# Head steps at half slots in a new order, tap responses in twenty chunks, and an eighth product with B on GpSimd

## The chip, the cores and the metric

The kernel runs on one core of one Trainium2 chip. The metric is the device time of one execution in microseconds (us). Lower is better.

## What is computed

The input is one image `x` of shape (1, 64, 256, 128): 64 channels, 256 time steps, 128 frequencies, in fp32. Two layers follow one another.

Layer 0 is a pair of bidirectional Mamba blocks, first along time (128 sequences of 256), then along frequency (256 sequences of 128). Every direction does this:

```python
xz = rmsnorm(u) @ in_proj.T ; x, z = split(xz)             # 128 + 128 wide
x  = silu(causal_conv4(x) + conv_b)
dt, B, C = split(x @ x_proj.T)                             # 4, 16, 16
dt = softplus(dt @ dt_proj.T + dt_b)
h  = exp(dt * A) * h + dt * B * x                          # scan, 128 x 16 states
y  = (h @ C + x * Dp) * silu(z)
out = y @ out_proj.T + u
```

The two directions are joined by a linear layer and added to the input.

Layer 1 normalises over the whole image (one mean and one deviation), runs a convolutional LSTM over 32 windows of 8 time steps in two directions, projects back, applies two PReLUs and adds the residual. The mean of the image enters the convolutions of layer 1 only through the response of each convolution tap to the norm's gain and bias; these "tap responses" need weights alone, so they can be made while layer 0 still runs.

## The kernel before

**Tiling.** `Stage` does one axis of layer 0: stage 0 along time, stage 1 along frequency. A stage has 64 chunks of 512 tokens. A chunk has two directions `d`, and a direction has 16 state groups of 128 rows, taken two at a time. Such a pair is one step `S` of the loop in `Stage.run`, so a chunk has 16 steps and a stage 1024. `where(S)` gives chunk, direction and group.

**One pair** (tiles of 128 partitions x 1024 fp32) goes through these methods:

- `inputs`: TensorE spreads `dtx` (dt times x) over the states into PSUM, tile `bx` (three buffers), line 445.
- `decays`: ScalarE takes `exp(A * dt)` from the loaded tile `rep` into SBUF, tile `dA` (line 468), and clears the column in front of each sequence (line 465).
- `times_b`: VectorE multiplies `bx` by B in place, in PSUM (line 480).
- `recur`: VectorE scans (line 490) into `h` (five buffers).
- `outputs`: GpSimd multiplies `h` by C (line 503).
- `add_up`: TensorE sums `h` over the states into `y` (line 512), once for two pairs.

For the pairs in `SWAPPED` (numbers within 32 pairs, two chunks) the two operands of the scan change places: ScalarE copies `bx` from PSUM into the `dA` tile (line 462) and puts the decays into the `bx` tile, and GpSimd does the product with B in SBUF (line 477). The scan then reads the decays from PSUM.

**The head.** What a chunk needs before its first pair is a list of steps, `HEAD`, written out by hand: each entry is a slot, a method's name and its arguments. Slot 16 is the chunk's own first step; slot 0 is 16 steps ahead of it. Slots below 0 and above 15 overlap with the neighbouring chunks. `load`, `squares`, `means`, `rms` and `normalise` make the normed input; `project_x`, `project_z` and `silus` make x and z of both directions; `project_bc` and `spread_bc` send B and C through DRAM to be spread over partitions; `softplus_a`, `softplus_b`, `softplus_sum` make dt; `dt_away` writes it to DRAM and eight `spread_dt` load it back, spread, into the `rep` tiles (seven buffers, `NREP`); `times_x` makes `dtx` on GpSimd (line 395).

**Order.** The schedule is manual: each engine runs its instructions in the order in which the program issues them, and each DMA here is issued by the SP queue in that same order. Within step `S` the program issues `times_b(S+1)`, `recur(S)`, the `gate` of a direction when it is done (line 528), `outputs(S-1)`, `inputs(S+2)`, `decays(S+2)`; then the head steps of that slot; then `skip`, `add_up`, `close_a`, `close_b`, `keep`. All projections, the softplus and the responses share one PSUM buffer, the tag "mm".

**Tap responses.** In stage 1 `Gates.fetch` loads the weights of one tap of one direction (512 KB, tile `w`, one buffer) at slot 10, and at slot 6 of the next chunk `Gates.respond` multiplies them with gain and bias: eight matmuls of two columns (line 707), which the profile records as sixteen, and one ScalarE copy into `made` (line 710). Ten chunks have one.

**After layer 0** `ConvLstm.prepare` combines weights and `ConvLstm.run` does the 32 LSTM steps. The change does not touch them.

Of the kernel before, what the change touches and what calls it, by code (L numbers as in the profile page):

```python
# [36 lines left out]
P = 128  # L37
# [19 lines left out]
HALF = T // 2  # L57
NRING = 4
NREP = 7
NH = 5  # L60
LAG = 2
SWAPPED = (3, 5, 10, 14, 19, 26, 29)
EXP_AND_LN = "natural_log_exp_and_others"
SILU = "silu_and_others"
EDGES = (0, 1, LF - 2, LF - 1)
# [1 line left out]


HEAD = (
    (-11, "load"),  # L70
    (-7, "squares"),
    (-5, "means"),
    (-5, "rms"),
    (-3, "normalise"),
    (0, "project_x", 0),
    (1, "project_z", 0),
    (4, "project_x", 1),
    (5, "project_z", 1),
    (5, "silus"),
    (6, "project_bc", 0),  # L80
    (8, "softplus_a", 0),
    (8, "softplus_b", 0),
    (10, "spread_bc", 0, 0),
    (10, "softplus_sum", 0),
    (12, "dt_away", 0),
    (12, "spread_bc", 0, 1),
    (12, "spread_dt", 0, 0),
    (12, "times_x", 0),
    (12, "spread_dt", 0, 1),
    (12, "project_bc", 1),  # L90
    (12, "spread_dt", 0, 2),
    (13, "softplus_a", 1),
    (13, "softplus_b", 1),
    (14, "spread_dt", 0, 3),
    (15, "spread_dt", 0, 4),
    (15, "softplus_sum", 1),
    (15, "spread_dt", 0, 5),
    (15, "spread_dt", 0, 6),
    (15, "spread_bc", 1, 1),
    (18, "dt_away", 1),  # L100
    (18, "spread_dt", 0, 7),
    (19, "spread_dt", 1, 0),
    (20, "spread_bc", 1, 0),
    (20, "spread_dt", 1, 1),
    (20, "times_x", 1),
    (22, "spread_dt", 1, 2),
    (22, "spread_dt", 1, 3),
    (23, "spread_dt", 1, 4),
    (26, "spread_dt", 1, 5),
    (27, "spread_dt", 1, 6),  # L110
    (27, "spread_dt", 1, 7),
)


# [118 lines left out]
class Stage:  # L233
# [8 lines left out]
    def __init__(self, ctx, m, stage, L, X, src, moments, gates):  # L242
# [8 lines left out]
        self.wk = ctx.enter_context(tc.tile_pool(name=n + "wk", bufs=1))  # L251
        self.st = ctx.enter_context(tc.tile_pool(name=n + "st", bufs=NH))
        self.dram = ctx.enter_context(tc.tile_pool(name=n + "dram", bufs=3, space=bass.MemoryType.DRAM))
# [162 lines left out]
    def spread_dt(self, ch, d, n):  # L416
        k, r = divmod(n, 2)
        t = self.wk.tile([P, 2, NTOK], F32, name="rep", tag="rep", bufs=NREP)
        there = self.at["there", ch, d]
# [28 lines left out]
    def swapped(self, S):  # L448


        return S % 32 in SWAPPED

# [125 lines left out]
    def run(self):  # L578
        nch = NCH
        last = 16 * nch  # L580
        silu = next(slot for slot, name, *_ in HEAD if name == "silus")
        steps = {}
        for ch in range(nch):
            for slot, todo in self.head(ch).items():
                steps.setdefault(16 * (ch - 1) + slot, []).extend(todo)
        for S in range(min(steps), last + LAG + 4):
            if 0 <= S + 1 < last:
                self.times_b(S + 1)
            if 0 <= S < last:
                self.recur(S)  # L590
            if S % 8 == LAG and S > 8:
                self.gate(*self.where(S - 8)[:2])
            if 0 < S <= last:
                self.outputs(S - 1)
            if 0 <= S + 2 < last:
                self.inputs(S + 2)

            for ahead in ((2, 3) if S % 16 == silu else () if S % 16 == silu + 1 else (2,)):
                if 0 <= S + ahead < last:
                    self.decays(S + ahead)  # L600
            for f, args in steps.get(S, []):
                f(*args)
            if S % 8 == LAG and 0 < S < last:
                self.skip(*self.where(S)[:2])
            if (S - LAG) % 2 and LAG < S <= last + LAG:
                self.add_up(S - LAG)
            if S % 16 == LAG and S > 16:
                self.close_a(S // 16 - 1)
            if S % 16 == LAG + 1 and S > 16:
                self.close_b(S // 16 - 1)  # L610
                self.keep(S // 16 - 1)
            if not self.time and S > 16:
                if S == last + LAG + 2:
                    self.spread_of(nch - 1)
                elif S % 16 == 14 and S < last:
                    self.spread_of(S // 16 - 1)

                n = S // 16 - 1
                if n < 10 and S % 16 == 10:
                    self.gates.fetch(n, self.io)  # L620
                if 0 < n < 11 and S % 16 == 6:
                    self.gates.respond(n - 1, self.mm("made"))


class Moments:
# [47 lines left out]
class Gates:  # L673
# [24 lines left out]
        self.w = pool.tile([P, 4, 256], F32, name="w", tag="w")  # L698
        self.nc.sync.dma_start(out=self.w, in_=self.d[("W_ih_f", "W_ih_b")[n // 5]][:, n % 5])

    def respond(self, n, pm):
        nc = self.nc
        half, k = divmod(n, 5)
        for gate in range(2):
            to = pm[:, 2 * gate : 2 * gate + 2]
            for j in range(4):
                nc.tensor.matmul(
                    to, lhsT=self.w[:, j, gate * P : (gate + 1) * P], rhs=self.gb, start=j == 0, stop=j == 3
                )
        nc.scalar.copy(  # L710
            self.made[:, 2 * half : 2 * half + 2, k], pm[:, 0:4].rearrange("p (g i) -> p g i", g=2)
        )


class ConvLstm:
# [449 lines left out]
```

## Time and profile before

| | before |
|---|---|
| median of 3 runs | 7435.62 us (7434.42 to 7440.39) |
| profiled execution | 7439.22 us, span 7437.4 us, mean TensorE clock 0.977 |
| VectorE (DVE) busy | 6987.4 us, 94% of the span |
| GpSimd (POOL) busy | 6558.7 us, 88% |
| TensorE (PE) busy | 6526.3 us, 88% (ends are modelled) |
| ScalarE (ACT) busy | 5999.8 us, 81% |
| first scan of stage 0 / stage 1 | 72.0 us / 3395.3 us |
| LSTM part | from about 6751 us to the end |

A line of the page's groups names the line of the code, the engine, the operation, the tile written and the tiles read, their sizes and how often; after the bar stand the busy time and the mean of one instruction in ns, and after the second bar how long the engine stood idle just before these instructions and which instruction ended most of that wait. A line of the timeline has the start and the length in us. A line of stretches has, for each engine, the busy time and in brackets the number of instructions, then the granted TensorE clock, the DMA share and the rate.

### The profile page before, as it was taken

The numbers are of one execution on the slowest core, as the hardware profiler recorded it, in microseconds if no ns is written. First come the engines' busy times: TensorE is split into PE (matmuls) and PEld (weight loads), VectorE is DVE, ScalarE is ACT, GpSimd is POOL, SyncE is SP. The second block draws the span as 40 slices with busy tenths as digits, with TensorE's granted clock in tenths as the row PEclk, the third lists the DMA queues.
The fourth block names the chain that finished last, engine by engine and source line by source line (L and its number), as shares of the span: only waits on it lengthen the run. The fifth ranks groups of instructions, "written<-read, shape, count | busy, mean of one in ns | idle before, by whom it ended". The sixth has DMA issues, their size and how long they took to land. (4 is left out here: it accounts for less than half of the span.)

```text
span 7437.4 us, 86153 instructions
## 1 busy us (share of the span) xinstructions
PE 6526.3 (88%) x25104; PEld 2203.8 (30%) x25104; DVE 6987.4 (94%) x4740; ACT 5999.8 (81%) x10892; POOL 6558.7 (88%) x3348
## 2 busy tenths in 40 slices
PE   7888888888888888887888888888888888888999
PEld 2222222222222222222222222222222222225887
DVE  6999999999999999996888999999999999996887
ACT  6888888888888888877777889888888888884333
POOL 5999999999999999996888999999999999995554
PEclk9999999999999999998999999999999999999999
DMA  5887888887888888876777877777777878782000
GB/s 148 207 208 205 205 210 204 207 207 202 206 207 204 206 205 205 206 185 163 190 184 186 204 201 202 203 208 201 201 204 202 208 197 205 205 203 72 15 15 16
DMA packets 509540, 1359.97 MB, mean 183 GB/s; under 512 B 75376, under 2 KB 133392, under 8 KB 509072
## 3 DMA queue, kind: packets, MB, share of 16 engines
q1 hardware_dynamic: 509072, 1354.46, 71.4%
q8 instruction: 205, 3.36, 0.2%
q14 instruction: 263, 2.15, 0.1%
HBM read 1228.34 MB, written 92.27 MB: 178 GB/s over the span
## 5 line engine op out<-in xcount | busy, mean ns | idle before, releaser
L503 POOL TENSOR_TENSOR h<-h,C 128x1024 f32<-128x1024 f32 x2048 | 4795.1, 2367 | 137.7 <-DVE h L490 120.1
L490 DVE TENSOR_TENSOR_SCAN h<-dA,bx 128x1024 f32<-128x1024 f32 x1600 | 3602.3, 2271 | 7.7 <-ACT dA L468 7.7
L445 PE MATMUL bx<-dtx,sel 64*128 64x512 f32 x8192 | 2368.3, 654 | 205.9 <-DVE h L490 205.7
L480 DVE TENSOR_TENSOR bx<-bx,B 128x1024 f32<-128x1024 f32 x1600 | 1940.8, 1213 | 251.0 <-PE bx L445 250.7
L468 ACT ACTIVATE dA<-rep,A 128x510 f32<-128x510 f32 (+1 forms) x3200 | 2117.0, 710 | 9.2 <-DMA rep<-there 6.0
L477 POOL TENSOR_TENSOR dA<-dA,B 128x1024 f32<-128x1024 f32 x448 | 1057.0, 2359 | 294.1 <-ACT dA L462 284.5
L445 PEld LDWEIGHTS bx<-dtx,sel 64*128 64x128 f32 x8192 | 640.4, 188 | 1857.4 <-issue 1045.8
L512 PE MATMUL y<-h,fold 128*32 128x512 f32 x8192 | 1119.0, 614 | 14.3 <-POOL h L503 7.6
L490 DVE TENSOR_TENSOR_SCAN h<-bx,dA 128x1024 f32<-128x1024 f32 x448 | 1021.0, 2279 | 2.5 <-POOL dA L477 1.3
L462 ACT COPY dA<-bx 128x1024 f32<-128x1024 f32 x448 | 450.7, 1006 | 251.3 <-PE bx L445 251.3
L468 ACT ACTIVATE bx<-rep,A 128x510 f32<-128x510 f32 (+1 forms) x896 | 617.4, 689 | 29.4 <-ACT bx L465 0.2
L401 PE MATMUL pb<-xs,xbc 128*32 128x512 f32 x512 | 291.4, 654 | 287.8 <-ACT xs L349 239.5
L327 ACT ACTIVATE xs<-px,cb 128x512 f32<-128x512 f32 x256 | 175.9, 687 | 372.9 <-PE px L326 372.9
L512 PEld LDWEIGHTS y<-h,fold 128*32 128x32 f32 x8192 | 167.3, 109 | 788.3 <-issue 432.0
L395 POOL TENSOR_TENSOR dtx<-dt,xs 128x512 f32<-128x512 f32 x256 | 326.8, 1276 | 62.2 <-ACT dt L383 62.2
L325 PE MATMUL px<-unp,g 128*128 128x512 f32 x512 | 292.7, 653 | 78.2 <-ACT X L561 35.8
L379 PE MATMUL pv<-w,ident 128*128 128x512 f32 x512 | 276.9, 623 | 91.1 <-ACT w L371 91.1
L358 PE MATMUL pv<-xs,wdt 128*128 128x512 f32 x512 | 290.0, 648 | 67.1 <-ACT bc L403 59.4
L379 PE MATMUL pv<-e,ident 128*128 128x512 f32 x512 | 290.0, 648 | 11.1 <-ACT e L362 7.8
L332 PE MATMUL pz<-unp,wz 64*128 64x512 f32 x512 | 268.2, 603 | 3.2 <-ACT xs L327 3.1
L326 PE MATMUL px<-unp,g 128*128 128x512 f32 x512 | 266.2, 601 | 0.0
L379 PE MATMUL pv<-lw,ident 128*128 128x512 f32 x512 | 262.7, 595 | 0.0
(190 smaller groups left out, 6887.6 us busy)
## 6 DMA issues: line engine op xcount, KB each, us to landing
rep<-there SPq DMA_DIRECT2D x2048, 512.0 KB
B<-away SPq DMA_DIRECT2D x256, 256.0 KB
there<-dt SPq DMA_DIRECT2D x1024, 64.0 KB
C<-away SPq DMA_DIRECT2D x256, 256.0 KB
unp<-xn SPq DMA_DIRECT2D x512, 64.0 KB
away<-bc SPq DMA_DIRECT2D x256, 64.0 KB
u<-in_x SPq DMA_DIRECT2D x128, 64.0 KB
out<-y SPq DMA_DIRECT2D x32, 256.0 KB
```

Source lines behind the costliest of these rows:

```text
L325: nc.tensor.matmul(self.seqs(px), lhsT=m.G1[i], rhs=self.unp[:, :, first : first + L], start=True, stop=False)
L379: nc.tensor.matmul(pv, lhsT=self.m.ident, rhs=t, start=False, stop=n == len(parts) - 1, skip_group_check=True)
L395: self.nc.gpsimd.tensor_mul(dtx, self.at["dt", d], self.at["xs", ch, d])
L401: self.nc.tensor.matmul(pb, lhsT=self.m.Wbc[2 * self.stage + d], rhs=self.at["xs", ch, d], start=True, stop=True)
L445: self.nc.tensor.matmul(bx[:, j], lhsT=self.m.sel[rows, r, k], rhs=dtx[rows], start=True, stop=True)
L462: nc.scalar.copy(dA.rearrange("p j n l -> p j (n l)"), bx)
L468: nc.scalar.activation(dA[:, j, :, live], self.seqs(rep[:, j])[:, :, live], AF.Exp, scale=m.A[:, i, g : g + 1])
L477: self.nc.gpsimd.tensor_mul(bx, bx, b)
L480: self.nc.vector.tensor_mul(bx, bx, b)
L490: self.nc.vector.tensor_tensor_scan(h.rearrange("p j n -> p (j n)")[:, step], dA[:, step], bx[:, step], 0.0, ALU.mult, ALU.add,)
L503: self.nc.gpsimd.tensor_mul(h, h, self.at["C", ch, d].unsqueeze(1).to_broadcast([P, 2, NTOK]))
L512: nc.tensor.matmul(y[32 * r : 32 * r + 32], lhsT=m.fold[:, k], rhs=hs[r % 2][:, r // 2], start=False, stop=k == NK - 1, skip_group_check=True,
```

## The change

`Stage.run` gets a second place for head steps, at the end of a step, after `keep`: an entry with slot `s + 0.5` is issued there. Many entries of `HEAD` are moved to other slots and some change order (`project_z` of the second direction now comes before its `project_x`; `project_bc` of the first goes from slot 6 to 7.5). `SWAPPED` has eight pairs instead of seven, at other places. `respond` does one gate at a time, four matmuls and one copy, at slot 6 of twenty chunks; `fetch` moves from slot 10 of ten successive chunks to slot 6 of every other chunk, after the response.

```diff
--- before.py
+++ after.py
@@ -57,9 +57,10 @@
 HALF = T // 2
 NRING = 4
 NREP = 7
+RESPOND = 6
 NH = 5
 LAG = 2
-SWAPPED = (3, 5, 10, 14, 19, 26, 29)
+SWAPPED = (2, 5, 9, 14, 18, 21, 25, 30)
 EXP_AND_LN = "natural_log_exp_and_others"
 SILU = "silu_and_others"
 EDGES = (0, 1, LF - 2, LF - 1)
@@ -67,48 +68,48 @@
 
 
 HEAD = (
-    (-11, "load"),
-    (-7, "squares"),
-    (-5, "means"),
-    (-5, "rms"),
+    (-13, "load"),
+    (-8.5, "squares"),
+    (-4.5, "means"),
+    (-4.5, "rms"),
     (-3, "normalise"),
     (0, "project_x", 0),
-    (1, "project_z", 0),
-    (4, "project_x", 1),
-    (5, "project_z", 1),
+    (1.5, "project_z", 0),
+    (4, "project_z", 1),
+    (5, "project_x", 1),
     (5, "silus"),
-    (6, "project_bc", 0),
+    (7.5, "project_bc", 0),
     (8, "softplus_a", 0),
-    (8, "softplus_b", 0),
-    (10, "spread_bc", 0, 0),
-    (10, "softplus_sum", 0),
-    (12, "dt_away", 0),
+    (8.5, "softplus_b", 0),
+    (8.5, "spread_bc", 0, 0),
+    (10.5, "softplus_sum", 0),
+    (10.5, "dt_away", 0),
+    (11.5, "times_x", 0),
     (12, "spread_bc", 0, 1),
     (12, "spread_dt", 0, 0),
-    (12, "times_x", 0),
     (12, "spread_dt", 0, 1),
-    (12, "project_bc", 1),
-    (12, "spread_dt", 0, 2),
+    (12.5, "project_bc", 1),
+    (12.5, "spread_dt", 0, 2),
     (13, "softplus_a", 1),
     (13, "softplus_b", 1),
-    (14, "spread_dt", 0, 3),
-    (15, "spread_dt", 0, 4),
+    (13.5, "spread_dt", 0, 3),
+    (14.5, "spread_dt", 0, 4),
     (15, "softplus_sum", 1),
-    (15, "spread_dt", 0, 5),
-    (15, "spread_dt", 0, 6),
-    (15, "spread_bc", 1, 1),
-    (18, "dt_away", 1),
-    (18, "spread_dt", 0, 7),
-    (19, "spread_dt", 1, 0),
-    (20, "spread_bc", 1, 0),
-    (20, "spread_dt", 1, 1),
-    (20, "times_x", 1),
-    (22, "spread_dt", 1, 2),
+    (15.5, "dt_away", 1),
+    (16, "spread_dt", 0, 5),
+    (16.5, "spread_dt", 0, 6),
+    (16.5, "spread_dt", 0, 7),
+    (17, "spread_dt", 1, 0),
+    (17.5, "spread_bc", 1, 0),
+    (19, "spread_dt", 1, 1),
+    (20.5, "times_x", 1),
+    (21, "spread_dt", 1, 2),
     (22, "spread_dt", 1, 3),
+    (23, "spread_bc", 1, 1),
     (23, "spread_dt", 1, 4),
-    (26, "spread_dt", 1, 5),
-    (27, "spread_dt", 1, 6),
-    (27, "spread_dt", 1, 7),
+    (24, "spread_dt", 1, 5),
+    (26.5, "spread_dt", 1, 6),
+    (26.5, "spread_dt", 1, 7),
 )
 
 
@@ -583,7 +584,7 @@
         for ch in range(nch):
             for slot, todo in self.head(ch).items():
                 steps.setdefault(16 * (ch - 1) + slot, []).extend(todo)
-        for S in range(min(steps), last + LAG + 4):
+        for S in range(int(min(steps)), last + LAG + 4):
             if 0 <= S + 1 < last:
                 self.times_b(S + 1)
             if 0 <= S < last:
@@ -609,6 +610,8 @@
             if S % 16 == LAG + 1 and S > 16:
                 self.close_b(S // 16 - 1)
                 self.keep(S // 16 - 1)
+            for f, args in steps.get(S + 0.5, []):
+                f(*args)
             if not self.time and S > 16:
                 if S == last + LAG + 2:
                     self.spread_of(nch - 1)
@@ -616,10 +619,11 @@
                     self.spread_of(S // 16 - 1)
 
                 n = S // 16 - 1
-                if n < 10 and S % 16 == 10:
-                    self.gates.fetch(n, self.io)
-                if 0 < n < 11 and S % 16 == 6:
-                    self.gates.respond(n - 1, self.mm("made"))
+                if S % 16 == RESPOND:
+                    if 0 < n < 21:
+                        self.gates.respond(*divmod(n - 1, 2), self.mm("made"))
+                    if n < 20 and n % 2 == 0:
+                        self.gates.fetch(n // 2, self.io)
 
 
 class Moments:
@@ -698,18 +702,14 @@
         self.w = pool.tile([P, 4, 256], F32, name="w", tag="w")
         self.nc.sync.dma_start(out=self.w, in_=self.d[("W_ih_f", "W_ih_b")[n // 5]][:, n % 5])
 
-    def respond(self, n, pm):
+    def respond(self, n, gate, pm):
         nc = self.nc
         half, k = divmod(n, 5)
-        for gate in range(2):
-            to = pm[:, 2 * gate : 2 * gate + 2]
-            for j in range(4):
-                nc.tensor.matmul(
-                    to, lhsT=self.w[:, j, gate * P : (gate + 1) * P], rhs=self.gb, start=j == 0, stop=j == 3
-                )
-        nc.scalar.copy(
-            self.made[:, 2 * half : 2 * half + 2, k], pm[:, 0:4].rearrange("p (g i) -> p g i", g=2)
-        )
+        for j in range(4):
+            nc.tensor.matmul(
+                pm[:, 0:2], lhsT=self.w[:, j, gate * P : (gate + 1) * P], rhs=self.gb, start=j == 0, stop=j == 3
+            )
+        nc.scalar.copy(self.made[:, 2 * half + gate, k], pm[:, 0:2])
 
 
 class ConvLstm:
```

## The prediction

> **What bounds the kernel now.** I read the page's busy line first, then its costliest groups, then the busy time in stretches of the span, then the timeline around the places where VectorE stands still.
>
> ```profile
> PE 6526.3 (88%) x25104; PEld 2203.8 (30%) x25104; DVE 6987.4 (94%) x4740; ACT 5999.8 (81%) x10892; POOL 6558.7 (88%) x3348
> ...
> L503 POOL TENSOR_TENSOR h<-h,C 128x1024 f32<-128x1024 f32 x2048 | 4795.1, 2367 | 137.7 <-DVE h L490 120.1
> L490 DVE TENSOR_TENSOR_SCAN h<-dA,bx 128x1024 f32<-128x1024 f32 x1600 | 3602.3, 2271 | 7.7 <-ACT dA L468 7.7
> L480 DVE TENSOR_TENSOR bx<-bx,B 128x1024 f32<-128x1024 f32 x1600 | 1940.8, 1213 | 251.0 <-PE bx L445 250.7
> L477 POOL TENSOR_TENSOR dA<-dA,B 128x1024 f32<-128x1024 f32 x448 | 1057.0, 2359 | 294.1 <-ACT dA L462 284.5
> L462 ACT COPY dA<-bx 128x1024 f32<-128x1024 f32 x448 | 450.7, 1006 | 251.3 <-PE bx L445 251.3
> ```
>
> VectorE leads, GpSimd is next. Over the whole span this is an average; the stretches separate it (busy time of PE, weight loads, VectorE, ScalarE, GpSimd with instruction counts, then granted clock, DMA share, GB/s):
>
> ```profile
> 1500.00:2000.00 500.00, 443.92 (x1662) 121.10 (x1660) 492.28 (x299) 434.75 (x774) 474.52 (x220) 0.98 0.81 206
> 3500.00:4000.00 500.00, 430.08 (x1600) 137.03 (x1604) 433.66 (x261) 390.00 (x726) 419.02 (x194) 0.92 0.73 188
> ```
>
> In the first, VectorE is busy 492 of 500 us: it is the bound. In the second it loses 66 us, and so does every other engine: something stops them all. Those are the chunks with tap responses (the `made` matmuls run from 3529.2 to 4055 us). The timeline of one of them shows it (start, length, what; in brackets the idle time before):
>
> ```profile
> 3525.77 1.04 PE L401 MATMUL pb<-xs,xbc 128*32 128x512 f32 x2 [1.86 <-ACT xs L349]
> ...
> 3529.22 3.57 PE L707 MATMUL made<-gb,w 128*128 128x2 f32 x16 [2.40 <-ACT bc L403]
> ...
> 3532.72 2.08 PE L445 MATMUL bx<-dtx,sel 64*128 64x512 f32 x4
> ...
> 3534.84 1.23 DVE L480 TENSOR_TENSOR bx<-bx,B 128x1024 f32<-128x1024 f32 x1 [7.11 <-PE bx L445]
> ```
>
> TensorE waits for silu, then for the copy of bc (the response takes the single "mm" PSUM buffer that `pb` has just filled), spends 3.57 us on sixteen matmul records, and only then makes the next bx, at half its usual rate (2.08 us for four, else 1.13). VectorE has stood still for 7.11 us.
>
> **Periods.** VectorE's gate (L528) starts once per half chunk, so every second start is one chunk. From 567.27 to 2047.88 lie 29 chunks: 51.06 us each. From 5041.68 to 6219.65 lie 23: 51.22. In the response stretch the starts are 3544.22, 3602.28, 3660.46, 3718.41, 3776.61: 58.1 each. Two chunks, the period of the swapped list, take 102.3 us, or 116.2.
>
> What each engine needs of it, from start-to-start distances (shorter than the listed durations, since neighbours overlap):
>
> ```profile
> 1036.40 1.21 DVE L480 TENSOR_TENSOR bx<-bx,B 128x1024 f32<-128x1024 f32 x1
> 1037.52 2.28 DVE L490 TENSOR_TENSOR_SCAN h<-bx,dA 128x1024 f32<-128x1024 f32 x1
> 1039.71 1.21 DVE L480 TENSOR_TENSOR bx<-bx,B 128x1024 f32<-128x1024 f32 x1
> ...
> 1040.06 9.31 POOL L503 TENSOR_TENSOR h<-h,C 128x1024 f32<-128x1024 f32 x4
> ```
>
> VectorE: product 1.12, scan 2.19, gate 0.58 (1027.01 to 1027.59). 25 x 1.12 + 32 x 2.19 + 4 x 0.58 = 100.4 us. So it stands idle 1.9 us of 102.3, nearly all for bx from TensorE. GpSimd: product with C 2.33 (9.31 / 4), product with B 2.31 (1006.34 to 1008.65), dtx 1.23, xn 0.69. 32 x 2.33 + 7 x 2.31 + 4 x 1.23 + 2 x 0.69 = 97.1 us, so it idles 5.2. The table of waits agrees: from 500 to 3300 us GpSimd waits 138.0 us, 5.0 per two chunks, of which 92.4 for ScalarE's copy (L462).
>
> [...]
>
> **The eighth swapped pair** (8 in 32 for 7). Off VectorE: one product, 1.12 us per two chunks; it needs 99.3. Onto GpSimd: 2.31; it needs 99.4. The two are level, so the floor falls from 100.4 to 99.4. Onto ScalarE: the copy 1.01, one bx zero column 0.17 and one dA zero column 0.19, since 24 pairs instead of 22 meet the condition, of which one is the bx: 1.4 us onto about 89 (434.75 of 500), which leaves 10. TensorE gets nothing. The scan takes 2279 for 2271 ns: nothing. The new list is spaced 3 to 5 pairs, the old 2 to 7; the pair 3, 5, which has VectorE running twice past GpSimd within two pairs, goes. A swapped pair lets GpSimd fall 4.64 - 2.19 = 2.45 us behind, and each ordinary pair gives 3.31 - 2.33 = 0.98 back; so three between them nearly balance it, and dtx and xn (6.3 us) use what VectorE's gates (2.3) and the rest leave. I keep VectorE's 1.9 us of idle time as it is: 99.3 + 1.9 = 101.2, 1.1 us less. Bounds: idle time gone, 99.4 (2.9 less); GpSimd keeps all 5.0 us of its waits, 104.4 (2.1 more).
>
> Steady chunks: 64 in stage 0 and 54 in stage 1, 59 double chunks x 1.1 = **65 us**. The ten former response chunks get it too: 5 x 1.1 = 5.5 us.
>
> **The responses.** Before: ten stops of 58.1 - 51.2 = 6.9 us, 69 us in all. The same 160 matmul records and the same ten fetches of 512 KB remain, as twenty bursts of eight, 1.8 us by the row above. They sit at slot 6, right after project_x of the second direction, whose ScalarE copy precedes the silus, and project_bc goes from slot 6 to 7.5. So the 2.40 us wait on bc is no longer in front of the burst, and the 1.86 us in which TensorE waited for silu now has the burst in it. Best: 0 per burst. Worst: the whole burst and one bx at half rate, 1.8 + 0.95 = 2.75. I take 0.9, a third, as three bx buffers cover part: 20 x 0.9 = 18, a gain of **51 us** (14 to 69). The ten added copies (0.16 us) lie on ScalarE. The fetch moves to slot 6 ahead of three transfers of the second direction (two rep of 512 KB and C of 256 KB) and must wait on SP for the burst that frees `w`. If all of it queues, C lands later by 512 KB at 206 GB/s, 2.5 us, ten times; C is asked for two slots (6.4 us) before its use, so I cost it at nothing, and 25 us if the cover is gone.
>
> **The head laid anew.** The order on GpSimd changes only for dtx of the first direction, one pair earlier (11.5). ScalarE's dt is then made at the end of slot 10 instead of its middle, so some 3 us of slack go; before, dt was done at 1030.28 and dtx began at 1033.49, so about nothing is left and nothing lost. dt_away goes ahead by 1.5 and 2.5 slots, which takes SP's wait for it (300 us from 500 to 3300) from in front of the rep loads: SP isn't the bound, nothing. The rep loads stay behind the freeing of their seven buffers (two later pairs of the second direction come half a slot sooner). project_bc off the silu's heels removes a 1.9 us stop of TensorE in every chunk, part of VectorE's idle time; half-slot places elsewhere may add as much. Taken as nothing; bounds are the 1.9 us of idle time, gone or doubled, 59 x 1.9 = 112 us either way. Stage starts (VectorE first runs at 66.6 and 3390.6 us) keep their chain; 5 us either way. The LSTM part is untouched.
>
> **Sum.** 65 + 5.5 + 51 = 121.5 us off the profiled execution's 7439.2 us (span 7437.4): 7317.7. The median of the runs shown is 3.6 us below that execution, so **7314 us**.
>
> **Rivals.** (1) Responses only: GpSimd, now level with VectorE, adds a wait for each one saved, and two chunks stay at 102.3. Then 51 us: 7385. For it: of 101.2 us neither VectorE nor GpSimd has 2 to spare. Against: GpSimd's waits for ScalarE come from being early, and a later GpSimd finds the copy done.
> (2) Slower: GpSimd becomes the bound because its waits for the copy stay. Place: L477, in its queue ahead of the product with C; behind it stand h, y and the h buffers, and VectorE's scan of that pair waits for it too. Price: 99.4 + 5.0 = 104.4, 59 x 2.1 = 124 us more, 51 back from the responses and 10 lost in the response chunks: 7435.6 + 83 = 7519. It decides from waits of 102.3 - 99.4 + 51 / 64 = 3.7 us per two chunks on; it has 5.0 now. For it: the copy needs bx early, and TensorE and ScalarE are near 88%. Against: the reason above.
> (3) Better: moving project_bc frees TensorE's stop, and idle time falls to 0.5: 99.9, 64 x 2.4 = 154, with bursts free 69: 7213.
>
> **Chances.** Forecast 0.60, (1) 0.18, (2) 0.15, (3) 0.07. A measurement of this kernel tells some 0.2% (15 us) from no change. Rival (2) in its weaker forms lies around no change, so: faster 0.82, same 0.04, slower 0.14. The forecast's own range is 7255 to 7375; up to (1) with some loss, **7250 to 7425** leaves out (2) and most of (3).
>
> **What would show it.** Right: L477 x512, L480 x1536; VectorE's gates 50.6 us apart on average; GpSimd over 97% busy in a steady stretch and its waits under 2 us per double chunk; `made` in twenty bursts with no wait on bc, VectorE's stops there under 1 us. Wrong: steady chunks at or over 51.2 with VectorE's scans waiting for L477, or bursts that still stop VectorE for over 2.75 us.

## The result and the profile after

The changed kernel takes 7356.72 us (median of 4 runs, 7348.72 to 7366.53) against 7435.02 before: ratio 0.9894, 95% interval 0.9877 to 0.9911, 78 us less. The profiled execution is the fastest of the four (7348.72 us, span 7346.9). The busy line and the costliest groups of the page after (line numbers are one higher than before):

```profile
PE 6503.7 (89%) x25104; PEld 2256.3 (31%) x25104; DVE 6918.5 (94%) x4676; ACT 6114.9 (83%) x11094; POOL 6702.8 (91%) x3412
...
L504 POOL TENSOR_TENSOR h<-h,C 128x1024 f32<-128x1024 f32 x2048 | 4796.9, 2365 | 33.4 <-DVE h L491 22.9
...
L481 DVE TENSOR_TENSOR bx<-bx,B 128x1024 f32<-128x1024 f32 x1536 | 1862.8, 1213 | 221.5 <-PE bx L446 221.3
...
L478 POOL TENSOR_TENSOR dA<-dA,B 128x1024 f32<-128x1024 f32 x512 | 1205.8, 2355 | 150.3 <-ACT dA L463 135.3
...
L463 ACT COPY dA<-bx 128x1024 f32<-128x1024 f32 x512 | 518.4, 1012 | 358.7 <-PE bx L446 344.4
```

The work moved as the diff says: 64 products went from VectorE to GpSimd. GpSimd's idle time in front of L478 and L504 fell from 432 to 184 us. VectorE's, in front of L481, fell only from 251 to 222 us, although the stops at the responses, 69 us before, are gone. The stretches tell the two apart (same columns as before the change):

```profile
1500.00:2000.00 500.00, 443.33 (x1666) 126.83 (x1670) 487.90 (x295) 446.80 (x796) 486.31 (x226) 0.97 0.80 205
3500.00:4000.00 500.00, 452.84 (x1763) 135.32 (x1763) 493.81 (x298) 459.49 (x856) 491.87 (x229) 1.00 0.82 212
```

The response stretch, VectorE 433.66 us busy before, is now the better of the two, at a granted clock of 1.00. In the steady stretch VectorE stands idle longer than before, 12.1 of 500 us where it was 7.7.

Chunk lengths from the starts of VectorE's gates give the account: stage 0 averages 51.01 us (51.08 before), the ten former response chunks 50.50 (58.08), the next ten, which now have a response too, 50.50 (51.49), the rest of stage 1 51.18 (51.17). The two profiled executions lie 90 us apart, more than the medians. Nearly all of it, 76 + 10 us, lies in twenty chunks, and the other 108, which were to bring 60 us, brought about 5.

The averages hide two kinds of chunk. Of the first 62 of stage 0, 23 take 50.1 to 50.2 us and the other 39 from 51.3 to 51.9. The trace also records the clock that TensorE was granted. By that record 38 of the 39 long chunks hold one stretch at half rate (a clock drop), and none of the 23 short ones does. (The 39th, from 3040.86 us, is long by a wait of 1.29 us of TensorE at px.) The kernel before has both kinds too: 22 of its 62 hold such a stretch and take 51.8 us on average, the other 40 take 50.7. Here is what the longer ones have after the change, from the timeline:

```profile
1010.78 1.01 ACT L463 COPY dA<-bx 128x1024 f32<-128x1024 f32 x1
...
1013.38 0.57 ACT L404 COPY bc<-pb 32x512 f32<-32x512 f32 x1
...
1014.00 1.69 PE L359 MATMUL pv<-xs,wdt 128*128 128x512 f32 x2 [1.83 <-ACT bc L404]
...
1015.62 2.08 PE L446 MATMUL bx<-dtx,sel 64*128 64x512 f32 x4
...
1017.75 1.23 DVE L481 TENSOR_TENSOR bx<-bx,B 128x1024 f32<-128x1024 f32 x1 [1.21 <-PE bx L446]
```

ScalarE comes out of the silus and runs, in program order, the copy and the decays of swapped pair 9 (slot 7) before the copy of bc (slot 7.5). TensorE's pv needs the mm buffer that bc still holds, waits 1.83 us, and runs at half rate after it: four bx records take 2.08 us for 1.13. The next bx is late and VectorE waits 1.21 us. Before, TensorE's stop stood at another place; the table of waits from 500 to 3200 us has the change (us in total, times, longest). First the kernel before, then after:

```profile
PE pb L401 <- ACT xs L349: 98.7, 53, 1.9
PE pv L358 <- ACT bc L403: 22.0, 27, 0.9
```

```profile
PE pv L359 <- ACT bc L404: 102.2, 65, 1.8
POOL dA L478 <- ACT dA L463: 50.3, 60, 1.2
```

The wait of pb for silu is gone from the list, and one of the same total has come at pv. Before, all 22 stretches at half rate followed the wait of pb (1.86 us); now all 38 follow the wait of pv. Chunks without such a stretch did become shorter, 50.7 to 50.1 us, but 16 more chunks have one. A response chunk looks otherwise:

```profile
3668.24 1.05 PE L709 MATMUL made<-gb,w 128*128 128x2 f32 x8
...
3672.37 1.04 PE L402 MATMUL pb<-xs,xbc 128*32 128x512 f32 x2 [0.70 <-ACT made L712]
...
3674.52 1.23 DVE L481 TENSOR_TENSOR bx<-bx,B 128x1024 f32<-128x1024 f32 x1 [0.27 <-PE bx L446]
3675.43 1.13 PE L359 MATMUL pv<-xs,wdt 128*128 128x512 f32 x2 [0.96 <-ACT bc L404]
```

The burst takes 1.05 us, pb waits 0.70 us for the copy of made, pv only 0.96 for bc; pv then runs at full rate (1.13 us).

### The profile page after: what moved, and what is told of

Same layout as the page of the kernel before. It is cut to its first block, busy times and chain, and to the rows that moved or that the text cites. A ratio compares the mean times of both kernels' runs of the same rounds, so it can differ in the third digit from the quotient of the medians.

```text
span 7346.9 us, 86550 instructions
## 1 busy us (share of the span) xinstructions
PE 6503.7 (89%) x25104; PEld 2256.3 (31%) x25104; DVE 6918.5 (94%) x4676; ACT 6114.9 (83%) x11094; POOL 6702.8 (91%) x3412
## 5 line engine op out<-in xcount | busy, mean ns | idle before, releaser
L504 POOL TENSOR_TENSOR h<-h,C 128x1024 f32<-128x1024 f32 x2048 | 4796.9, 2365 | 33.4 <-DVE h L491 22.9
L491 DVE TENSOR_TENSOR_SCAN h<-dA,bx 128x1024 f32<-128x1024 f32 x1536 | 3443.6, 2269 | 4.4 <-ACT dA L469 4.4
L446 PE MATMUL bx<-dtx,sel 64*128 64x512 f32 x8192 | 2565.9, 650 | 384.3 <-DVE h L491 382.5
L481 DVE TENSOR_TENSOR bx<-bx,B 128x1024 f32<-128x1024 f32 x1536 | 1862.8, 1213 | 221.5 <-PE bx L446 221.3
L469 ACT ACTIVATE dA<-rep,A 128x510 f32<-128x510 f32 (+1 forms) x3072 | 2021.6, 711 | 5.8 <-DMA rep<-there 5.6
L478 POOL TENSOR_TENSOR dA<-dA,B 128x1024 f32<-128x1024 f32 x512 | 1205.8, 2355 | 150.3 <-ACT dA L463 135.3
L446 PEld LDWEIGHTS bx<-dtx,sel 64*128 64x128 f32 x8192 | 730.8, 189 | 1896.0 <-issue 1070.9
L513 PE MATMUL y<-h,fold 128*32 128x512 f32 x8192 | 1236.6, 615 | 12.3 <-POOL h L504 11.8
L491 DVE TENSOR_TENSOR_SCAN h<-bx,dA 128x1024 f32<-128x1024 f32 x512 | 1167.8, 2281 | 11.3 <-POOL dA L478 11.3
L463 ACT COPY dA<-bx 128x1024 f32<-128x1024 f32 x512 | 518.4, 1012 | 358.7 <-PE bx L446 344.4
L469 ACT ACTIVATE bx<-rep,A 128x510 f32<-128x510 f32 (+1 forms) x1024 | 705.6, 689 | 33.7 <-ACT bx L466 0.4
```

What stands on the lines that cost most here:

```text
L446: self.nc.tensor.matmul(bx[:, j], lhsT=self.m.sel[rows, r, k], rhs=dtx[rows], start=True, stop=True)
L463: nc.scalar.copy(dA.rearrange("p j n l -> p j (n l)"), bx)
L469: nc.scalar.activation(dA[:, j, :, live], self.seqs(rep[:, j])[:, :, live], AF.Exp, scale=m.A[:, i, g : g + 1])
L478: self.nc.gpsimd.tensor_mul(bx, bx, b)
L481: self.nc.vector.tensor_mul(bx, bx, b)
L491: self.nc.vector.tensor_tensor_scan(h.rearrange("p j n -> p (j n)")[:, step], dA[:, step], bx[:, step], 0.0, ALU.mult, ALU.add,)
```

## The experiments

Theory: the steady chunks lost the gain at one place, pair 9's copy ahead of bc on ScalarE, through TensorE's clock. Rival: VectorE and GpSimd are level and hand each saved wait back. All times are medians; "before" ran beside them at 7434 to 7439 us. "Of 62 at half rate" counts the first 62 chunks of stage 0 within which the granted clock fell to a half.

| run | us | ratio to before (95%) | chunk in stage 0 | of 62 at half rate | ten first response chunks |
|---|---|---|---|---|---|
| before | 7435 | 1 | 51.08 | 22 | 58.08 |
| changed kernel | 7357 | 0.9894 (0.9877 to 0.9911) | 51.01 | 38 | 50.50 |
| e1 burst in every chunk | 7344 | 0.9868 (0.9853 to 0.9882) | 50.75 | 28 | 50.68 |
| e2 seven pairs | 7343 | 0.9863 (0.9849 to 0.9878) | 50.74 | 13 | 50.78 |
| e3 whole bursts | 7377 | 0.9914 (0.9899 to 0.9929) | 51.02 | 36 | 51.67 |
| e4 half bursts alone | 7470 | 1.0037 (1.0024 to 1.0049) | 50.97 | 17 | 56.38 |
| e5 bc at 6.5 | 7410 | 0.9963 (0.9950 to 0.9975) | 50.61 | 0 | 54.56 |
| e6 pairs 10, 26 for 9, 25 | 7250 | 0.9748 (0.9734 to 0.9761) | 50.09 | 0 | 50.24 |
| e7 eight pairs alone | 7585 | 1.0196 (1.0183 to 1.0210) | 52.24 | 40 | 58.85 |
| e8 burst and copy in every chunk | 7295 | 0.9806 (0.9793 to 0.9820) | 50.43 | 0 | 50.70 |
| e9 head alone | 7355 | 0.9895 (0.9878 to 0.9911) | 50.72 | 12 | 51.85 |
| e10 burst ahead of pb alone | 7411 | 0.9967 (0.9954 to 0.9980) | 50.99 | 19 | 55.51 |
| e11 old head, 10 and 26 | 7440 | 1.0004 (0.9996 to 1.0013) | 51.01 | 13 | 57.92 |
| e12 nine pairs | 7350 | 0.9886 (0.9872 to 0.9901) | 50.83 | 18 | 51.13 |

**e1, a burst in every chunk.**

```diff
+            if S % 16 == RESPOND and 0 <= S < last and (self.time or not 0 < S // 16 - 1 < 21):
+                self.rouse(4)      # four matmuls ident x gb into mm("rouse"), not read
```

> The changed kernel with four more matmuls of two columns (identity by gain and bias, their product unused) at slot 6 of every chunk that has no tap response, in both stages, so that all 128 chunks have the burst that twenty have. Theory (TensorE's clock): an ordinary chunk takes 50.1 us in stage 0 when TensorE keeps its clock and about 51.5 when it drops to half during the 1.83 us wait of pv (L359) for the bc copy; the chunks with a response took 50.5 us each at a granted clock of 1.00. With the burst everywhere nearly all chunks should take 50.1 to 50.5, so 64 x 0.8 in stage 0 and 44 x 0.7 in stage 1 go: about 82 us, 7275 us. Rival (GpSimd and VectorE, now level, hold each other up): more matmuls give nothing, 7357 us, or cost up to 108 x 0.3 = 30 us more.

Measured 7344, much nearer to the rival than to the theory. Clock drops became rarer (28 of 62 chunks where 38 were), but stayed. TensorE's timeline of a chunk with one says why:

```profile
4823.58 1.05 PE L582 MATMUL rouse<-gb,ident 128*128 128x2 f32 x8
...
4830.71 1.13 PE L359 MATMUL pv<-xs,wdt 128*128 128x512 f32 x2 [2.11 <-ACT bc L404]
4831.77 2.07 PE L446 MATMUL bx<-dtx,sel 64*128 64x512 f32 x4
```

The burst ran, pv still waited 2.11 us, and the clock fell (four bx records in 2.07 us). So my account of the response chunks was wrong in one point: it isn't the burst alone that helps. What a response has beyond it is ScalarE's copy, for which pb waits.

**e8, the burst and its copy.** The same with `nc.scalar.copy(self.spare, pm[:, 0:2])` after it.

> The four extra matmuls of every chunk without a response as in the first of these runs, with ScalarE's copy of their product to a spare tile added, as a response has it. The extra matmuls alone left pv waiting 2.11 us and the clock dropping in half of the chunks; in a response chunk pb first waits 0.70 us for the copy of made and pv then only 0.96. Theory (one long wait drops the clock, two short ones don't): with the copy all chunks take 50.1 to 50.5 us, 7280 to 7300 us. Rival (the other weights or the fetch of a response make the difference): as without the copy, 7344 us.

Measured 7295, as the theory said: 55 of 62 chunks are below 50.95 us, and no chunk has a stretch at half rate. The other seven are long by other waits of VectorE for bx, of 1.22 to 1.89 us. TensorE's timeline of a short one:

```profile
1516.14 1.04 PE L402 MATMUL pb<-xs,xbc 128*32 128x512 f32 x2 [0.41 <-ACT spare L587]
...
1519.20 1.12 PE L359 MATMUL pv<-xs,wdt 128*128 128x512 f32 x2 [0.96 <-ACT bc L404]
1520.26 1.13 PE L446 MATMUL bx<-dtx,sel 64*128 64x512 f32 x4
```

Added work of no use, 61 us faster than the changed kernel: pb comes later, the one long wait becomes two short ones, the clock stays (four bx records in 1.13 us; mean granted clock 0.995, 0.976 in the changed kernel).

**e5, bc ahead of pair 9.**

```diff
-    (7.5, "project_bc", 0),
+    (6.5, "project_bc", 0),
```

> The changed kernel with project_bc of the first direction at slot 6.5 instead of 7.5. In the changed kernel ScalarE has, at slot 7, the copy of bx and the decays of the swapped pair 9 (or 25) ahead of the bc copy; pv waits 1.83 us for bc, TensorE's clock halves after it, and the next bx comes 1.2 us late. Theory (that one wait): at 6.5 the bc copy stands in front of pair 9, pv finds the buffer free, the clock stays, and ordinary chunks take 50.1 to 50.5 us: 85 us off, 7275 us. In the twenty response chunks pb then waits for the copy of made with a bx behind it, up to 20 x 1 us back: 7275 to 7295 us. Rival (VectorE and GpSimd, level, hold each other up): the stops move elsewhere, 7345 to 7365 us, as the changed kernel.

Measured 7410, slower than the changed kernel, and outside both expectations. Half of the theory holds: in stage 0 all 62 chunks take 50.6 us, without a clock drop. But what was saved came back in other places. Waits of VectorE and TensorE from 500 to 3200 us:

```profile
DVE h L491 <- POOL dA L478: 23.8, 54, 0.5
PE y L513 <- POOL h L504: 88.8, 54, 1.7
PE pb L402 <- ACT xs L350: 55.5, 54, 1.0
```

With bc first, pair 9's copy is late for GpSimd, VectorE's scan waits for the product once in each chunk, 0.44 us on average, and `y` waits for GpSimd. In stage 1 that wait of `y` is 1.84 us, clock drops follow it in 19 of the last 41 chunks, and outside the responses nothing is gained there (51.16 us a chunk). In the response chunks the head's half slot comes before the response, so the old order is back (burst waits 2.40 us for bc) and they take 54.6 us; I had the order there the wrong way round in the expectation. Either order of the two copies costs something, which suggests that the pair itself is in the wrong place; e6 tests that.

**e6, another pair.**

```diff
-SWAPPED = (2, 5, 9, 14, 18, 21, 25, 30)
+SWAPPED = (2, 5, 10, 14, 18, 21, 26, 30)
```

> The changed kernel with the swapped pairs 9 and 25 replaced by 10 and 26; the number of swapped pairs stays eight. Theory (the copy of pair 9 ahead of the bc copy): the wait of pv shrinks to about 0.8 us, as in the run with seven pairs where it was that long, the clock mostly stays, and two chunks take 100.2 to 101 us: 40 to 85 us off, 7275 to 7320 us. Rival (level engines): the spacing is less even (5 after 5, 21 to 26), VectorE waits for GpSimd more, and it is at or above 7357 us.

Measured 7250, better than the best that was expected, and 106 us under the changed kernel. Every chunk of the first 62 is below 50.95 us and none has a clock drop; stretch and waits (500 to 3200 us):

```profile
1500.00:2000.00 500.00, 442.35 (x1696) 126.44 (x1692) 496.11 (x300) 452.52 (x799) 494.77 (x230) 1.00 0.84 210
```

```profile
PE pv L359 <- ACT bc L404: 43.7, 108, 0.6
```

pv's longest wait is 0.6 us, the clock is whole, VectorE and GpSimd are both 99% busy. The rival falls: two level engines can both be kept full.

**e12, nine pairs**, `(2, 5, 10, 13, 17, 20, 23, 26, 30)`.

> The changed kernel with nine swapped pairs in 32, evenly spaced and none at 9 or 25: 2, 5, 10, 13, 17, 20, 23, 26, 30. By the sum VectorE needs 98.2 us per two chunks and GpSimd 99.4 + 2.3 = 101.7. Against the run with eight pairs and 10, 26 (100.2 us per two chunks, 7250 us) GpSimd is then the bound: 64 x 1.5 = 96 us slower, 7346 us, with VectorE's scans waiting for L478. If GpSimd was not near its limit at eight, nine is as fast or faster: 7180 to 7250 us.

Measured 7350, the sum said 7346. GpSimd is the bound (a stretch, and a wait from 500 to 3200 us):

```profile
1500.00:2000.00 500.00, 445.77 (x1674) 125.55 (x1672) 487.55 (x292) 452.51 (x802) 499.50 (x232) 0.99 0.82 207
```

```profile
DVE h L491 <- POOL dA L478: 23.2, 56, 0.7
```

499.5 of 500 us. Eight is where the two meet, as the prediction had it.

**e2, seven pairs**, the old `SWAPPED` in the changed kernel.

> The changed kernel with the old list of seven swapped pairs: head and responses changed, the swap not. Clock theory: the eighth pair is worth the 1.1 us per two chunks that VectorE loses of work (50.1 against 50.7 us a chunk), in disturbed chunks as well, since the stop comes on top: 64 x 1.1 = 70 us slower than the changed kernel, 7427 us. Rival (level engines): the eighth pair is worth nothing because each saved product becomes a wait of the two; then 7357 us, the same as the changed kernel.

Measured 7343: at these places the eighth pair makes the kernel 14 us slower by the medians (the two intervals just touch), where 70 us faster or no change were expected. Neither holds. Without a drop, two chunks take 100.8 us (50.8 + 50.0) with seven pairs and 100.3 with eight; but seven have drops in 13 of 62 chunks and eight in 38. The 13 follow another wait, of 1.81 us, in which TensorE waits for VectorE's scan to free a bx buffer. Work saved, stops added.

**e7, eight pairs alone**, the new `SWAPPED` in the old kernel.

> The kernel before with the new list of eight swapped pairs and nothing else. If the eighth pair is worth what its work is (1.1 us of VectorE per two chunks), it takes 59 to 70 us off: 7370 us. If it is worth nothing because it only turns work into waits of TensorE, ScalarE and GpSimd, as the run with seven pairs and the rest of the change says, it takes 7435 us or more. In the old head bc is copied at slot 6, ahead of pair 9, so the clock theory expects no new stop at pv here.

Measured 7585, much slower. The old head copies bc first, so pair 9 is late:

```profile
1566.40 0.57 ACT L403 COPY bc<-pb 32x512 f32<-32x512 f32 x1
...
1566.88 1.00 ACT L462 COPY dA<-bx 128x1024 f32<-128x1024 f32 x1
...
1567.95 2.35 POOL L477 TENSOR_TENSOR dA<-dA,B 128x1024 f32<-128x1024 f32 x1 [1.73 <-ACT dA L462]
...
1570.34 2.29 DVE L490 TENSOR_TENSOR_SCAN h<-bx,dA 128x1024 f32<-128x1024 f32 x1 [1.32 <-POOL dA L477]
```

Two chunks take 104.5 us; the prediction's second rival put 104.4 on it, by this chain: GpSimd waits for the copy at L477, VectorE's scan behind it. Clock drops cost nothing visible here: the 40 chunks with one average 52.27 us, the 22 without 52.20.

**e11, the old head with 10 and 26.**

> The kernel before with the list that has 10 and 26 in place of 9 and 25, head and responses old. With 9 and 25 the old head took 7585 us: the copy of pair 9 comes late behind the silus, so GpSimd waits 1.7 us for it and VectorE's scan 1.3 us for GpSimd. If pair 9 is the cause, 10 and 26 take it away and the eighth pair brings its 1.1 us per two chunks: 7365 to 7400 us. If the old head can't feed eight pairs wherever they are, 7480 us or more.

Measured 7440, between the two. The list with 10 and 26 takes 145 us off the 7585, so pairs 9 and 25 were that much of it. But it is no faster than seven pairs: of 62 chunks 49 take about 50.7 us, the length of undisturbed chunks before, and 13 with a clock drop 52.3; responses still take 57.9. The old head gives nothing for the eighth pair. From 500 to 3200 us pb still waits for silu once in each chunk, 1.8 us, and VectorE waits 46.4 us for bx, where e6, with the same list and the new head, has 18.9 and no wait of pb.

**e9, the head alone**, seven pairs and old responses.

> The kernel before with the new head and its half slots alone: seven swapped pairs, ten bursts of eight at slot 6, fetch at slot 10. If the new head's place for project_bc is what frees the responses, this run is already near the run with head and new responses (7343 us), worse by what whole bursts cost under the eight pairs (16 to 20 us): 7360 us. If the small bursts carry the gain, it keeps most of the 69 us of the old stops: 7410 us or more.

Measured 7355: the head by itself gives 79 us, as much as the whole change. Response chunks fall from 58.08 to 51.85 us with whole bursts, stage 0 from 51.08 to 50.72.

**e3, whole bursts in the changed kernel.**

> The changed kernel with the old responses: ten bursts of eight matmuls at slot 6 and the fetch back at slot 10; the new head and the eight pairs stay, so the burst stands in its new place (after project_x, ahead of project_bc) at its old size. Theory: the place counts. The burst of 3.6 us no longer follows the waits for silu and bc; it costs 1 to 2 us in each of ten chunks, and the other ten lose the burst that keeps the clock up, 10 x 0.7: 7357 + 15 + 7 = 7379 us. Rival (size counts): each burst still stops VectorE for about half of what it did, 10 x 3.5 = 35, so 7357 + 35 + 7 = 7399 us or more.

Measured 7377, as the theory said: the half bursts are worth 20 us here.

**e4, half bursts alone in the old kernel.**

> The kernel before with the responses alone changed: twenty bursts of four matmuls at slot 6, where the old head has project_bc just in front. Theory (place counts): each burst still waits 2.4 us for the bc copy and takes 1.8 us, and TensorE's clock still drops, so each stops VectorE for about 3.5 to 4.5 us: 70 to 90 us for twenty against 69 for ten before, 7435 to 7455 us. Rival (size counts, and a half burst falls under the cover of the three bx buffers): under 1 us each, 7435 - 69 + 20 = 7386 us.

Measured 7470, worse than expected: twenty response chunks of 56.4 to 56.5 us, 5 us more each than chunks without one. Where pb sits just in front, halving the burst only doubles the number of stops.

**e10, whole bursts ahead of pb alone in the old kernel.**

> The kernel before with one move: the ten whole bursts are issued ahead of the head steps of slot 6, so ahead of project_bc, and nothing else. If the wait for the bc copy in front of the burst is the cost (place), most of the 69 us goes, less 1 to 2 us per burst and the wait of pb for the copy of made: 7380 to 7395 us. If the size of the burst is the cost, at most the 2.4 us of the wait goes ten times: 7412 us.

Measured 7411, with the size side. Response chunks fall only from 58.1 to 55.5, by the 2.4 us of the wait and little more. One of them in the timeline:

```profile
3526.42 1.91 PE L401 MATMUL pb<-xs,xbc 128*32 128x512 f32 x2 [3.02 <-ACT made L711]
3528.26 2.08 PE L445 MATMUL bx<-dtx,sel 64*128 64x512 f32 x4
...
3530.39 1.23 DVE L480 TENSOR_TENSOR bx<-bx,B 128x1024 f32<-128x1024 f32 x1 [5.05 <-PE bx L445]
```

Now pb, ahead of the next bx in the same slot, waits 3.02 us for the copy of made, which ScalarE does after the silus. So it isn't which of the two comes first that counts; I take the cause to be that both stand in one slot. The new head puts pb one and a half slots later, and with it whole bursts leave response chunks of 51.85 us (e9).

## Why the prediction was right, and where its steps were not

Direction and range held: 78 us faster, 121.5 forecast. That the two lie this near is partly luck. The twenty response chunks brought 86 us of the profiled time where 62 were forecast (51, and 1.1 for each two of them), the steady ones about 5 where 60 were, and the errors partly cancel.

**Responses, 51 us (14 to 69), and 5.5 from the swap.** Mechanism right, too small. Ten chunks went from 58.08 to 50.50, 76 us. The term mis-sized is the 0.9 us per half burst: VectorE's stop there is 0.27 us, and a response chunk is 0.1 to 0.3 us longer than an undisturbed one (e6: 50.24 and 50.37 against 50.09). The burst took 1.05 us; I had 1.8 from a row in which TensorE ran at half clock (granted 0.50 over its 3.57 us; at the full clock a whole burst took 1.95 in e10). The second ten chunks gained another 10 us. The feared delay of C behind the fetch showed in no wait.

**The head laid anew, "taken as nothing", bounds 112 us either way.** Wrong step. Alone it gives 79 us, of which some 62 lie in the ten response chunks (e9). I had named the cause, project_bc off the silu's heels, and counted its part in the responses' wait under the responses, but not seen that their gain is nearly all the head's own: the half bursts alone cost 30 us in the old head (e4) and are worth 20 in the new one (e3). In the prediction's sum it thus appears under another name.

**The eighth pair, 65 us.** This is the step that failed: "I keep VectorE's 1.9 us of idle time as it is". The work did leave VectorE: two chunks of stage 0 without a clock drop went from 101.4 to 100.3 us, 0.6 of it by the head (e2: 100.8). But the 1.9 us were not a fixed idle time. They held the cost of clock drops in 22 of 62 chunks, the change made them 38, and the idle time of the average rose to 102.0 - 99.3 = 2.7 us. I compared the spacing of the pairs and not what else ScalarE has in those slots: pair 9, in both chunks of the list, has its copy at slot 7, directly behind 4.8 us of silus and table loads. e6 moves just those two pairs by one and gets 93 us over seven pairs (7250 against 7343), more than I asked. Only part of this is the pair's work: without drops two chunks take 100.2 us in e6 and 100.8 with seven (e2); the rest goes with the drops that seven pairs have (13 chunks of stage 0) and e6 has not.

**GpSimd level at 99.4, the bound at nine.** Right: e12 and e6 show both sides.

**The rivals.** (1) had the steady chunks unchanged, and on average they were, but by a stop of TensorE and not by GpSimd, whose waits fell from 5.0 to 2.6 us per two chunks ((50.3 + 9.1 + 6.6 + 2.7) / 26.5). (2) is real in the old head, at its price; the new head is what keeps it away. (3), 7213 us, is what the list with 10 and 26 comes near to (7250).

**The tests named.** L478 x512 and L481 x1536, twenty bursts with no wait on bc, stops under 1 us, GpSimd over 97% (486.31 of 500): as said. GpSimd's waits under 2 us per double chunk and chunks of 50.6 us: not met (2.6 and 51.0). The steady chunks of stage 1, at 51.18 us, stood at the line drawn for wrong, but VectorE's scans waiting for L478, which belonged to that sign, did not show.

**Shown and not shown.** That the long wait of pv costs the gain is shown by three ways of removing it (e5, e6, e8), all without a clock drop in stage 0, and by the record of the clock, in which 38 of the 39 long chunks hold a drop. Not every such wait brings one. Two chunks of stage 0 with the same wait of 1.83 us (TensorE's timeline):

```profile
352.90 1.12 PE L359 MATMUL pv<-xs,wdt 128*128 128x512 f32 x2 [1.83 <-ACT bc L404]
353.95 1.13 PE L446 MATMUL bx<-dtx,sel 64*128 64x512 f32 x4
...
403.04 1.72 PE L359 MATMUL pv<-xs,wdt 128*128 128x512 f32 x2 [1.83 <-ACT bc L404]
404.68 2.08 PE L446 MATMUL bx<-dtx,sel 64*128 64x512 f32 x4
```

After the first wait the granted clock is 1.00 (352.90 to 355.08 us), after the second 0.50 (404.68 to 406.76). What tells the two apart was not shown.

Not shown: pv, pb and the bursts wait for one another at a single mm buffer, and no run gave it a second one. What else, beside the wait of pb, keeps the eighth pair from paying in the old head (e11) was not separated.

## What to carry to other kernels

Before a product is moved to another engine, look at every engine that it touches at that slot, not only at the two that trade: here one copy on ScalarE, right behind the silus, turned the 65 us of VectorE time that were to be saved into a stop of TensorE. When a schedule is changed in several places, run each part alone and all but each: the parts alone (head, responses, eighth pair) gave -79, +30 and +148 us, and -78 together. An average idle time can hide two kinds of chunk: split it before a sum carries it over. And the length of a single wait can count: here chunks with one wait of pv of 1.83 us averaged 51.01 us, 38 of 62 with a clock drop, and chunks with two of 0.41 and 0.96 us averaged 50.43 with none (e8).

## What the runs showed of the hardware

- Four bx records took 2.08 us at a granted clock of 0.50 and 1.13 at 1.00 (after, from 404.68 and 353.95 us).
- Half rate followed a single wait of 1.8 us in some chunks and not in others: 1.86 us at pb in 22 of 62 chunks (before), 1.83 at pv in 38 (after), 1.81 at bx in 13 (e2). Two waits of 0.41 and 0.96 us 2 us apart brought none (e8).
- A burst of eight two-column records, ended 4 us before a wait of 2.11 us, didn't hold the clock up (e1): the four bx records after the wait took 2.07 us.
- GpSimd's products kept their length with VectorE 99% busy beside them (2366 and 2360 ns in e6, 2367 and 2359 before).
